# A context tile loaded by one transfer instead of two, with a new instruction order, in an attention and feed-forward kernel

## The chip, the cores and the metric

The kernel runs on one core of a Trainium2 chip. The metric is the device time of one execution in microseconds (us). Its engines are named as in the profile: PE (matrix multiplication; PEld is its weight load), DVE (vector), ACT (activation), POOL (general purpose), SP (here it only issues transfers). Each engine works through its own list of instructions in order and waits on semaphores for the others.

## What is computed

The reference, cut to what matters: x has 8 batches of 512 rows of 512; the context has 64 rows of 512 for each batch.

```python
xn = layernorm(x)
scores = einsum('bsd,bmd->bsm', xn, ctx) / sqrt(512)
attn = softmax(where(mask, scores, -1e30))
x = x + einsum('bsm,bmd->bsd', attn, ctx)          # 0 where a batch has no valid row
z = layernorm(x)
linear_bit(z, w, g) = act_quant(rmsnorm(z, g)) @ ternary_quant(w).T
h = silu(linear_bit(z, w1, g1)) * linear_bit(z, w2, g2)      # 2048 wide
x = x + linear_bit(h, w3, g3)
```

act_quant scales a row by its largest absolute value and rounds to 8 bits; ternary_quant needs the mean of |w| over the whole matrix (1 M values each) before a single weight can be rounded.

## The kernel before, in words

The head of the program brings the weights into shape. Each weight comes as four pieces of 1 MB (load_w, L315; tiles raw). measure_w (L339) sums |w| of each piece (L353), PE adds the partial sums over the partitions (pm, L363), DVE turns the mean into a scale (ws, L366 to L371). quantise_w (L379) scales and rounds a piece (tq, L386 on POOL or L387 on ACT), PE turns it (pw, L396), DVE clips it into w1T, w2T or w3T (L390). arctanh (L423) computes a factor from the mean in many instructions on one column (L434).

Per batch there are three stages. pre (L543) normalises x (statistics L560, t L582/L586), splits it into two float16 halves (xh: cast L590/L591, rest L592), transposes them (xT; on PE for batch 0, by a DMA transpose, L298, for the others), and multiplies by the context (psc, L602). expo and post (L631, L651) do the softmax and add the readout (po, L683; L691). quantise_x (L701) normalises again (xm, L721/L725), multiplies by g1 and g2 (z, L736), finds the largest values (zf, L741), rounds (L799/L800) and transposes (zT). Then, for each of four row blocks, gate and up (L891, L903) multiply by w1 and w2 (L883), apply Silu (L899), multiply both (L927), square (L932) and multiply by g3 (L940); the result is reduced (L964), rounded (L997/L999), transposed (hT) and multiplied by w3 (pd, L825) some blocks later. The last block ends in L854 to L866.

The context of a batch is wanted twice, on partitions 0 to 63 and again on 64 to 127, since the second half serves the low float16 part of the readout. load_x (L469) issues it: `both` (L473) holds the contexts of two batches and serves measure_mem (L489), which finds their scale; `mem` (L475 to L479) holds the one context in both halves; split_mem (L528) turns mem into `ms` (L533 on ACT, L536 on DVE) and its transpose mT. mem has two buffers, x and raw and h share nine large ones (BIG), matmul results share three buffers of two PSUM banks (mm).

The order of the work is written out. The Python code records operations (op, L108), many with several engines to choose from, each with cost estimates in ns; a string (ORDER, L151) holds a compressed list of numbers, each an operation and the engine it goes to, and Plan.order (L128) reads it. The numbers of the cost estimates are not used when the kernel is built: order and engines come from the string alone. All plain loads and stores and all DMA transposes are issued by SP, one after the other.

Of the kernel before, what the change touches and what calls it, by code (L numbers as in the profile page):

```python
# [87 lines left out]
class Plan:  # L88
# [19 lines left out]
    def op(self, engine, cost, run, writes, reads, table=None, other=()):  # L108

        me = len(self.ops)
        deps = set()
# [6 lines left out]
        for b, part in map(pair, writes):  # L120
# [28 lines left out]


ORDER = """  # L151
c-jTQedKy+q5$yo@|^eQob#M>o^#G~UY3@Y?~m_~mM$$_y0o;kv@~?-($LV*(9*qHS{k~vG&D4{S3{SEhW==1XlUqOEnONKS{fQ!8d_R
f`lF@cem)c>QkVi1q!1OQa#WtmQU!`oMe2nrQ4#8uDpMg<p<+~=s!|CmNu{VXm7(g?h3-;Ux=r<{4%MJ;G^9VFn$&>8^oJCphZLbl)KB
QIs2bI$BlOqQXH=A4QFnSkPpCEZhMrOz>R;$BHKS(ikp3k-r{2;TdPnW47@egL)RZ03-%}GdPUq+oHKxy0p8h*^p%V0+dQewtLMQ1TsV
V)Wzo3^a#XxpWQ*?p;mIh3b7MT(a8N>j3L1RXw-=p{Roc*3AOvpr-1O0nuNmu9$^C!AWpXey_!mMb-PPqkprr%*Ubed_<Ev7~{=~pJkZ
0Ri1qA~lR+jN|%(;Yg&beSYW*c4M>a!i{E*)DzLip+}b(F-QR9=Ir51R3xy^M>s(HRc0m!@S4TnI7}X_L&$vWJ};b**!O4TA;z?K^#n&
&zKqaCG$R00DopWU?}$3-?42lWV&F)WWk#4vtKhgFl7ep$Kb$p_&!)MBQ^ozY>OX&HS-12VaM#JV8b@qEz@PMpv||~5m<vUn1LO$Wko^
aCZG(COj`I0GY1J42|qA@W0LF!U?Ihh#2x#0Ce3DqP|vVX$g(t>74FQF*@7IK6CTW-&9i_lu<r;vP-HL6ci_NEY>7RxW%k5Y*n%(xXZF
HY*(10}PjF=mTv0fI8(U-VY@L0uG4Nz7;2rJ^y22a&p8@13um?9#1!e9eA+E>)`2z0Xw*Ye~PzM99!oB4l0Dv?&aaB$PPbtPNK%A>_ge
wV45OPB<#X%6^5QuVft}HY_f;)3>xSmiEk{kv^Xo6pHRiVUPI09CH;#yo^7zrWBa#yL!i*f`2uFV~U92W%(?#k7<SN<rxfF<_|R$PbsB  # L160
}egRsliclL|=0UzQzxPE%$p)<N^O8oP-#^6}#LUdBeTRJ09{+zR!&XN<jQXXbL?J2zx#zr}-Oa^E>X&J(N(0^J_6KKe&z9<wHKhzo=^=
%lG&sAK~Xhf`4*Rekj)ksOI<-KjQLyLn!haf$&42z>m3=^eRq;_xKWj;?v?n_#I#8D`JK3^Plofe!_LcwKU>q!XNpiu#sv)34P8d<drb
yqvH2`SBwZV{wy@a8$ac5%8Qtk@5)p7nxFGnEs1~Q-wG*t!T(HH^G$T;FG5@dVp-hqq7s$P{FZ<4P#MVyk&-AeE{S4HxbR8wA&zAzUIi
jH#gsUa3sPK&sX3`7hT=_#t9RiS!c%-zcOp^$A^Z;?5!+}iHlz=Qw(ufVq;G_s&=J~VUTR86-3v)!DZNTn=_noLln|2+;#`V}C;292#J
!jok78Dwi0`N;aVi$XAH<nxh#gcxTdANH#f4;xWz<4dloQYLT`H<j-bqNgihmW~RjVSBKS%$k?xlxx7i;1ag>p@*i#HKSJuxEN(nr!vh
SCg0Wl`#jL>h=UIU)7rP(l)x=VDD>iVJZi-sOy(lp<0~p2~HpE;r=0e34U9T1v}TIG0y)QNqfvq>}WI`_hL}TPjPhN>(CrSzX9ixg&*2
Oxdaf={t!iznAAqMCnOcxuWLesM1ina#dX@Z8-{uQd7yxDWxFil(aID{#(i@9i=aK<gz@Kwn|r7$}?#o$F(M`$O&zyY~+?wmACR(+AD9
AfzpCE*oOt>Tlo%qN?tiAOXVqNbV^C<M`ZwCAW(Afr0mqVvX>J|Q7$U4@Tu%oQ7b8Z<y|=st4awbmG_i{`o8jO1;CnekSTbANv*E56{v
l#i116)hC>Cykz&B9V#6`?;7mEg2b{pH{+SZO3q;xzifRP@#Guqr<<ylDQKRZcIjC#ptfaK08iz4BR8ug8x>gz{;8jVf8TF!+VMZINSv
3QbFsDw{u^KUE))3aziB*B2mW5bLs|DD%(pnWpv<0leqgq$z*3|k4)?o)`wGo`c9=xhE*i@rhPMgDmwm?O=REc&{=h|0lRXeLoxPoJ?0  # L170
axnhYC|t-6Rn}H;Z5DZnYz&S@T9fWwR(UL?V_HwwmMgP>Jiqoi~iK^YF?{reU;M3`a^AMPnFVMwSoE#>{;K!7j0nuL7i&9)7n~7k7+<(
YfCMvU$lw7(^pzYn`wKitmX8LCh9NxN9tC4)puGJMGdI$^@85gUW~og(%;oO#zBjtiZ<1OwnSI`sLl1fo<LpgW38yCQ4OuoK>If%hYnT
-mGp!DiT0iz(`Wk8s-uTK)ZW*t`c-@CBdv=*GHzPWC>eGAu61;zxAh(x=rz5suTc`+^sY|yzJc`{%A<u2QNyg8OTDM}Q4!V5ve7_yv_Y
ThuLd%PsAAl8${6W2V}w?E+8CpOvC-?spY)-D(EuIwlO8hwI_o2YLIotEszFfPc%YOqb+&rK*rFY37zn9G(wG`!BWs4}N3=&X<AC0vjd
MnEb7kzDxr2>Y^f1;&!rU1f<ELor#L&;s-pQGw`80rWMa0OPWAlQbd9pG_28+hTpiE>goTr&JW=_tSm`(G0ls7&!n#RE(=2r$~wT*9#q
&YYC#?CC5cV}rFjlZCi@q_VK1DHkgYV6H|fh}y7%!3)4cOzmpEMmQwM>C6W#@ULRB`dVr=Bqh1TV~8mSUKD=KQ`lf*F2e@m<c_pr}VNF
v4Ax&o7T{}SShP&rOc5zvcAM2zFH5bgVScxD&mZp#}S;h($@c)bF*d*&4u-axiL$4ZPu-f)x~GCY%Z<5wJ@XB*4*HgRj^*H9$uOYe6xy
H%PQcDSv4zG*ID8|zM4;`V<qv;Y+Ds`Y^^Y~?xtvMth@Ca>lGtwh__b7{kipO?W_;no>RtA9JgxtVXmzz9^t+-z`wv-JjRs!u%h<U+Tj
WYZrpycpP0fDe!&2%7~vEy*$ErthF!K}IE@KD;HG`EYwi)Z>^QFD(3!Y<+`vh@iCcJWPw~*6;I<9yh%>{l_Qp=zqI<%3dyUUH?xbw!?%
gXE?Hj)1ihaQer(^#E*WIz*#!H8?M>eu!Hnyj3%X!D{+65ch8GGgy?TMYWR}ONg_80b-_Q3hhox8uW+m2^1?5#a?4$jdH?U56)tM<|9*  # L180
-N`_FWiAmIcNK1pWMEEv6t@2so5+0TN}GccW)o;tG#lg4safJ+DW;hbF>@o*-1KQH{)Df=s<#;g7fNp=5(B#({!)y8z<|eoR|~3H+SOX
owZYRpLWZ=IKOi9<m$9tL~`!U!Op+BEmCr_ZplrPo||{mE+)h&J7u@%v`N>!yK6T?D$c--xF0wnIg`3mAjIvvQTL5IAaC6w>9|9;;f&m
koAjE_kZj!xp~=pT5|8A)lvg4n@^A|t^2X%p=E#y1y$Z>a7lJ)NN?w`7T#>BF$Q!%Fi@Ph*AyxA4WJ79BjWo#AOSoIo@V+IX_h&Npnq=
i2$jpn7rZ*uiZ|!ZpDd~C@zvsP@wzu<sK{{TS{G3$%e<GiFSCS-s67hNjcqx+fY41kvMDmVg?xnq`_aG+%y|TCW1|IS&-i!AnLvP_tJn
Ub*S1;zxNZiYKDSzozy<dA9@8Hcz&O3Sw67gGp+CO=}^={tTi}?w!?p;0NXZ*MR!EgI_Z|mp$xZm*~-j5#b1Apvi{m@VNHNWfce9^!9M
<4n<KkDE7sh<c=e&5ggg&-Nc_!Ix^&-`*w@aKLpDEeRdU;7RJKm5JF@+-l+e$#*WpZfphm;Gum^3%c7uLWzL3NC&o*!Z&m1li#3Hv=)q
1tb^;Fff93&<Z9&JHSCScnNU03Fbj0Bw;5AgKiKBJ`VmEd=e~zT@VdlgJm!bQo%kL1?lh*<b&^nQt-Fn9^8UNI0%#BBcQ`)z=cv+4>I8
}Yy_h)8^UlJyo9+h7L3DkxC&4>3Ae%9Fdm$Od{_x*;WRu4^Dq`(f-qc!)vy*e!g|;YTVXuxhN-X}_QF4eg|Htk!(zAzOW`WqhU@SU?!t
X|3{T-X{D0au@s|
"""  # L190
# [953 lines left out]
```

## Time and profile before

| | |
|---|---|
| runs | 428.87 us median of 3 (427.7 to 428.94) |
| profiled execution | 427.9 us, of which the profile's span is 425.8 us |
| PE busy | 388.8 us (91%), 2174 matmuls |
| DVE, ACT, POOL busy | 369.0 us (87%), 341.3 us (80%), 368.7 us (87%) |
| granted TensorE clock, mean | 0.987 |
| read from memory, written | 25.76 MB, 8.39 MB |
| the chain that ended last | 78% PE, 6% DVE, 6% POOL, 3% DMA |

The profile is of one execution. Its page gives the busy time of each engine, the span in 40 slices (tenths of a slice, clock, transfer rate), and groups of instructions by line of the kernel with their mean duration and what they waited for; the trace behind it gives the same for any stretch, and instructions in order of time. Idle time on an engine that doesn't set the end costs nothing.

### The profile page before, as it was taken

The numbers are of one execution on the slowest core, as the hardware profiler recorded it, in microseconds if no ns is written. First come the engines' busy times: TensorE is split into PE (matmuls) and PEld (weight loads), VectorE is DVE, ScalarE is ACT, GpSimd is POOL, SyncE is SP. The second block draws the span as 40 slices with busy tenths as digits, with TensorE's granted clock in tenths as the row PEclk, the third lists the DMA queues.
The fourth block names the chain that finished last, engine by engine and source line by source line (L and its number), as shares of the span: only waits on it lengthen the run. The fifth ranks groups of instructions, "written<-read, shape, count | busy, mean of one in ns | idle before, by whom it ended". The sixth has DMA issues, their size and how long they took to land.

```text
span 425.8 us, 6677 instructions
## 1 busy us (share of the span) xinstructions
PE 388.8 (91%) x2174; PEld 192.8 (45%) x2174; DVE 369.0 (87%) x832; ACT 341.3 (80%) x464; POOL 368.7 (87%) x330
## 2 busy tenths in 40 slices
PE   0563878999999999999999999999999999999996
PEld 0341534544444544454445444544454444444444
DVE  4689999999998998799989998999789888897772
ACT  1799999979899799598996898988686986774531
POOL 1789998998999999699999999999699979988650
PEclk9996899999999999999999999999999999999999
DMA  7999994497555578863589635864644546533272
GB/s 217 408 406 376 380 208 52 103 255 147 126 112 150 99 131 157 183 174 68 104 158 276 136 76 82 171 174 83 134 76 148 75 87 146 152 77 73 49 207 90
DMA packets 142514, 67.35 MB, mean 158 GB/s; under 512 B 133136, under 2 KB 133520, under 8 KB 140048
## 3 DMA queue, kind: packets, MB, share of 16 engines
q1 hardware_dynamic: 142480, 66.93, 63.4%
q8 instruction: 17, 0.28, 0.3%
q14 instruction: 17, 0.14, 0.1%
HBM read 25.76 MB, written 8.39 MB: 80 GB/s over the span
## 4 chain that ended last, share of the span: by engine, by line
PE 78%; DVE 6%; POOL 6%; DMA 3%; issue 3%; ACT 2%; SPq 0%; DVEq 0%; POOLq 0%; ACTq 0%
PE p L883 48%; PE pd L825 24%; PE po L683 3%; DMA zT<-xm 2%; PE psc L602 2%; POOL tq L386 2%; DVE st L560 1%; DMA both<-in_ctx_dram 1%; PE pd L854 1%; POOL t L586 1%; POOL xh L592 1%; POOL mv L291 1%; DVE zf L741 1%; DVE h L927 1%; ACT h L899 1%
## 5 line engine op out<-in xcount | busy, mean ns | idle before, releaser
L883 PEld LDWEIGHTS <-zT 128*128 128x128 f16 x1024 | 99.5, 98 | 122.0 <-issue 3.0
L940 POOL TENSOR_TENSOR h<-h,g_bc 128x1024 f32<-128x1024 f32 x55 | 130.4, 2377 | 2.7 <-ACT sq L932 2.1
L883 PE MATMUL p<-w1T,zT 128*128 128x512 f16 x512 | 120.4, 383 | 2.4 <-DVE zT L309 1.5
L883 PE MATMUL p<-w2T,zT 128*128 128x512 f16 x512 | 119.2, 379 | 1.1 <-DVE h L927 0.9
L825 PE MATMUL pd<-w3T,hT 128*128 128x512 f16 x496 | 117.8, 379 | 0.0
L927 DVE SCALAR_TENSOR_TENSOR h<-p,zf,h 128x1024 f32<-128x1024 f32 x64 | 81.9, 1280 | 14.9 <-PE p L883 8.4
L899 ACT ACTIVATE h<-p,zf 128x1024 f32<-128x1024 f32 x64 | 70.1, 1105 | 24.8 <-PE p L883 17.0
L932 ACT ACTIVATE sq<-h 128x1024 f16<-128x1024 f32 x64 | 67.2, 1050 | 17.0 <-DVE h L927 14.8
L825 PEld LDWEIGHTS <-hT 128*128 128x128 f16 x496 | 47.9, 98 | 55.6 <-DMA hT<-h 0.2
L964 DVE TENSOR_REDUCE hf<-h 128x1 f32<-128x2048 f32 x31 | 70.6, 2278 | 1.8 <-POOL h L940 1.7
L736 POOL TENSOR_TENSOR z<-xm,g_bc 128x1024 f32<-128x1024 f32 x29 | 69.8, 2423 | 1.4 <-ACT xm L725 0.6
L997 ACT ACTIVATE h<-h,hf 128x2048 f16<-128x2048 f32 x23 | 45.8, 1994 | 0.2 <-DVE hf L968 0.2
L741 DVE TENSOR_REDUCE zf<-z 128x2 f32<-128x1024 f32 x32 | 38.8, 1211 | 5.8 <-POOL z L736 5.7
L592 POOL TENSOR_TENSOR xh<-t,xh 128x512 f16<-128x512 f32 x32 | 37.3, 1168 | 2.0 <-DVE xh L591 1.2
L799 ACT ACTIVATE xm<-z,zf 128x512 f16<-128x512 f32 x42 | 28.1, 709 | 0.7 <-DVE zf L760 0.7
L731 ACT ACTIVATE xsq<-x,xf 128x512 f32<-128x512 f32 x32 | 22.9, 715 | 6.5 <-DVE x L691 6.0
L835 DVE SCALAR_TENSOR_TENSOR x<-pd,hf,x 128x512 f32<-128x512 f32 x31 | 23.1, 744 | 3.0 <-PE pd L825 2.6
L691 DVE SCALAR_TENSOR_TENSOR x<-po,mx,x 128x512 f32<-128x512 f32 x32 | 22.9, 745 | 1.3 <-PE po L683 1.2
L602 PE MATMUL psc<-mT,xT 128*128 128x128 f16 x256 | 19.7, 224 | 1.9 <-DMA xT<-xh 1.9
L560 DVE BATCH_NORM_STATS2 st<-x 128x6 f32<-128x512 f32 x32 | 21.3, 679 | 0.0
L602 PEld LDWEIGHTS <-xT 128*128 128x128 f16 x256 | 16.9, 101 | 8.5 <-DMA xT<-xh 3.5
L291 POOL TENSOR_TENSOR hf<-hf,neg_half 128x1 f32<-128x1 f32 x32 | 20.1, 634 | 0.2
(134 smaller groups left out, 483.4 us busy)
## 6 DMA issues: line engine op xcount, KB each, us to landing
raw<-in_L_ffn_w_dram SPq DMA_DIRECT2D x10, 1024.0 KB, 13.8
x<-in_x_dram SPq DMA_DIRECT2D x7, 1024.0 KB, 6.9
out_dram<-x SPq DMA_DIRECT2D x7, 1024.0 KB, 4.1
mem<-in_ctx_dram SPq DMA_DIRECT2D x16, 128.0 KB, 6.5
w3T<-in_L_ffn_w_dram SPq DMA_DIRECT2D x2, 1024.0 KB, 12.6
both<-in_ctx_dram SPq DMA_DIRECT2D x4, 256.0 KB, 8.2
x<-in_x_dram SPq DMA_DIRECT2D x2, 512.0 KB, 6.1
g_bc<-in_L_ffn_g_dram SPq DMA_DIRECT2D x1, 1024.0 KB, 14.9
```

The costliest lines, as they stand in the source:

```text
L592: rest = lambda e, t=t, xh=xh: e.tensor_tensor(xh()[:, 1, :], t(), xh()[:, 0, :], ALU.subtract)
L602: T.matmul(psc()[:, c, :, :].rearrange("p s m -> p (s m)"), xT()[:, k, :], mT().rearrange("p (s d) m -> p d s m", s=2)[:, k % ND, :, :], s ...
L736: gain = lambda e, xm=xm, z=z: e.tensor_tensor(z(), xm().broadcast_to([P, 2, D]), g_bc(), ALU.mult)
L741: lambda i=i, z=z, am=am: V.tensor_reduce(am()[:, i, :], z(), AX.X, ALU.max, apply_absolute_value=True),
L825: T.matmul(po(), hT()[:, n * P : (n + 1) * P], w3T()[:, n, :], start=(n == 0), stop=(n == NH - 1),)
L883: T.matmul(ps()[:, k * HC : (k + 1) * HC], zT()[:, g * ND + d, :], weight(d, j * HW // HC + k), start=(d == 0), stop=(d == ND - 1),)
L899: lambda: A.activation(h()[:, j * HW : (j + 1) * HW], ps(), AF.Silu, scale=fac()[:, 0:1]),
L927: lambda: V.scalar_tensor_tensor(cols(), ps(), fac()[:, 1:2], cols(), ALU.mult, ALU.mult),
L932: lambda: A.activation(sq(), cols(), AF.Square, scale=(RMS / H) ** 0.5, accum_out=col(j)),
L940: run = lambda e: e.tensor_tensor(cols(), cols(), g3_bc()[:, j * HW : (j + 1) * HW], ALU.mult)
L964: lambda: V.tensor_reduce(col(2), h(), AX.X, ALU.max, apply_absolute_value=True),
L997: op(ACT, 1995, lambda: A.activation(hq(), h(), AF.Copy, scale=col(5)), [h], [(f, 5)], other=[(POOL, 1970, lambda: G.tensor_scalar(hq(), h ...
```

## The change

There are three parts. First, the two transfers of 64 partitions each become one, whose source names the same 64 rows twice. Second, the order string is another one; its text is left out here. Third, some cost estimates change, which has no effect on the program by itself.

```diff
@@ load_x
         mt = plan.buffer(att, "mem", [P, D], F32, 2, f"mem_{b}")
-        for half in range(2):
-            op(DMA, (475, 650, 364, 500),
-               lambda half=half: Q.dma_start(mt()[half * M : (half + 1) * M, :], mem[b]),
-               [(mt, half)], [])
+        op(DMA, (475, 650, 700, 500),
+           lambda: Q.dma_start(mt(), mem[b : b + 1].broadcast_to([2, M, D])),
+           [(mt, 0), (mt, 1)], [])
@@ load_w, constants, quantise_w: estimates
-            op(DMA, (475, 650, 2750, 1400), lambda k=k: load(k), [raw[i, k]], [])
+            op(DMA, (475, 650, 2620, 1400), lambda k=k: load(k), [raw[i, k]], [])
...
-               other=[(POOL, 1970, lambda by=by: by(G)), (DVE2, 1700, lambda by=by: by(V))])
+               other=[(POOL, 1970, lambda by=by: by(G)), (DVE2, 1275, lambda by=by: by(V))])
...
-        op(DMA, (475, 650, 730, 800), lambda g=g, src=src: Q.dma_start(g_bc()[:, g, :], ...
+        op(DMA, (475, 650, 1160, 800), lambda g=g, src=src: Q.dma_start(g_bc()[:, g, :], ...
```

In the built program the source of a mem transfer, before, is 64 rows of 512 values, twice; afterwards it is 2 copies (step 0) of 64 rows (step 512) of 512 values, and its destination 128 partitions of 512 values.

What the new order does, told from the lists of instructions of each engine:

- SP: both, half of x, mask, half of x, mem, then w1's pieces (second, third, first, fourth), w2's four pieces with the two g_bc transfers among them, the next batch's mem, x and both, three pieces of w3, mem and x of batch 2, the last piece of w3, x of batch 3, both, mem of batch 3, the transposes mT and xT of batch 1, then g3. Before: mask, both, the two halves of mem and x in turn, w1, g_bc, w2 and g_bc, x and mem of batch 1, two pieces of w3, both, a piece of w3, g3, x of batch 2, the last piece of w3, mem.
- ACT: ms of batch 1 (L533) stands ahead of the last half piece of w2's measure; xm of row block 0 (L725) is made here and no more on POOL.
- DVE: one piece of w1's measure (L357), 11 more products h by g3 (L940, 20 for 9), 6 more products z (L736, 9 for 3), 4 rests xh (L592, none before); fewer small columns.
- POOL: 44 for 55 products L940, 23 for 29 products L736, 28 for 32 rests L592; more small columns.
- PE: the same instructions in a slightly other order; the first scores of batch 1 (L602) stand ahead of the fourth turned z of batch 0 and of the sum pm of w3.

More of the change, by code (lines that the diff above doesn't have):

```diff
@@ L151 @@
 ORDER = """
[L152 to L186, printed above, removed]
@@ L187 @@
-1tb^;Fff93&<Z9&JHSCScnNU03Fbj0Bw;5AgKiKBJ`VmEd=e~zT@VdlgJm!bQo%kL1?lh*<b&^nQt-Fn9^8UNI0%#BBcQ`)z=cv+4>I8
-}Yy_h)8^UlJyo9+h7L3DkxC&4>3Ae%9Fdm$Od{_x*;WRu4^Dq`(f-qc!)vy*e!g|;YTVXuxhN-X}_QF4eg|Htk!(zAzOW`WqhU@SU?!t
-X|3{T-X{D0au@s|
+c-jrp{pYf2q5$ygzVGXPf4lDY>wXy;S{nMHhn9wh9$H#jS~@gzXlQAUmWCdh)f^2C4GlfCe4nGCb2RirLqkJDOG8UTOG`sTOG6J04GsO
+!(qZ@WH+%qqAPhK=1189WEGU8qD1j&_fHJ^90s%M?EpQ=XpaUwP4Z0u%UV<~h5q<Ck;$Q&21_^+OB=`oTfJyuXR6z|OAQ3~b1a;6Sz5o
+rd0xmHI0g(n*B1B9;n0SY1f(&?0M2IzbMWl%l)gz`LN@R!)h!I<`16g8B4Tv8=oX8OeFeH8kN01<{;0E%<h&X`}%~50GPJBrehzD^8Md
@@ new lines @@
+AUb#NUV+F`-JtmY7n2{DFYv8I%b?%n6Q!#B)+2>%@UTWSXoH4Z<X=1SY>FYQ&8CklYa)8c{hiAe+R3$dD4%B38ta*wT4&PBqCk(IVG`N
+oC0t#8imv5CyVJ1k`_$pORHFOukRH$r<?`StGk-h>DP5DoRDDC>f)&@QHds#mG9@BO5RZzaryg4mOw;{FqvieKHTb)R<0?|4SBNmrIgu
+*o0+rK&9b=`i87C8Q7+V)Ti(ZvJ2zXf*g}E_;>OZ*@H`RN%g1>^=G&y`&5H^f-7o3HmNZjz&o>m3F-tl<c=J|FG+$<QV(WNCfOyt5&s~
+Ia80GC9``eurcx|aGZbKdA}26QtzewJlUFiFCD=SQf*b1p$u+!@KavFsvVba5Te#zY!)~bzOH(CkN0q4~RiXA&l{!!xeg{ufj=sSfwTE
+Xa0xwhv{u*xJ0iI!zhIAQbS&qK)d3r}@>Gz>TUtj{3=qkLzqj-c@DhYdZj-7KKu~9nDBKlW!ndaC6+ovORku~WG9iwmj6k>W$Pv{y9=o
@@ new lines @@
+TBNXRr?6q!09SdJgY!&rj(R(`Ii}nts3n-JsWOlRoo3HpILpXLO6cQ%9OpxBP>u(ic8M16ZTi41{yK%y95VOK?HI!C>}5cUVgZGgxTT8
+}<dgWbX8m?$TTK!gT1jm@2zsVoZX0O-Gp~bEdD%O}fy1_Qn7PLCDNl69xieW}L((=-)CJCYdt(#F|V1vrLOgF_?LxD{Kg+nH4=^<IIE)
+!z&#U5c>|DW7hPXEwTT>bXg=<m;w7oCg8?wn|YUsb2X+T4Cz-)ft&IZcE>ijBGYB2?2w)DJ;vn1LZ3M@118KxgoB8=e=wgiIj$=_q@UR
+<JD^Vt&kUIg*ArxB#5B1vW3e+P!u^ezGdC9Td2Yunm@RW=qTHU13U9DC;m)2oQ;u<I^kAzT$L*O57h=zx#2wfWA7)GFEp{y=d6Vx8AFw
+rU!hFjf**Y6#(|n3Qu?-f;W&SJXC-yF3zRvZzJdd~vpFvqP=0jY8kFjZP%`eytmqS?I2tz*Lv)mJR7gpSgJ@5-|zy<P>tDq4-=O03XTX
@@ new lines @@
+RYI$ZxnRO37uE<WBsaTku=q&ZoG~5W#J^BA=EITo2J)k$dn<{<rdxYjGux6Uy9;yK)C%$TfI^?{Iex@@;M^kGMV>2$BE<j(>1SC<;~Kd
+v454xT7%Te#J|CS!fCoz9f|RCn3tm_?Q61i7*v1d|Vg`S^gyany>OXzQtn^3Y?ggcS4O1#F0?v6Fd}~yd)0AoczAf=8@RpYeHTwiz9I_
+%!G<q7ZbvV!cJ-lbFt5trLi!RpZEd)SN;tpDa_?x<j?q*d`id&bs;IHg@%|D7NR8Og|@I1=fXmWiWi|N#l*7^7cCJ<SD_;9rGk(aS7KA
+FiU+AJhQzQq7T*>_N<>_XDKRG|q`bHhqiRiD$Sui~mO@6%NLle?u^?8Zq_h&k%3A7+Me!m6tt*wpqx4GLNLMi{oWz0H5zk^*yvb0$iFf
+fNy%gILA;r|5be2N$UH*3zc_LmUC~c*wSdeF8AYG-09F`xVD@pQO(wkC5UdmfBqQs=I^n_w^O4^A~sTxr!D#zuR5|=n7Aw#Vw=cT>)JE
@@ new lines @@
+<?X<(xE>;>rNME7hc)0hAX~SMJC~DJ?amvK&?V(oTMoR&qiaNF%9ZbR<bx%PFO94CRg7RmM_D8p|)`fzng@#zdM*B{{7uq$l~P<dvZ^l
+9$p%UMpcVL|;oQ=>vHn{~#CDjdGB?#t2p9qg<6=%MJOYY~{XkmOE-eF_orVRFLwHGEvS7R^C%KYE>zz7o{bSl&w<LYD!$~s#j$$jg^^N
+R&L6Z(lD~hRFTw~vQWxuQq3q!1*3|xQZ6#5%~ho4lqa=j)RmdhPy+Nqj-Z7qX<Kz}w3LJTT#KQj`hnI{+e$*+DH%16zEL_#U(KVGx-b$
+bucy_$5=AwXQx8gA`!6+w{-mb0f?7a#C8OolrkX-Eb*C257**94YG@y;J5<nt`nft(P4%H5ZLii*UOS<zhSj#(KrJna_NcC!+DN^sWA&
+zfq%74oYNC~TR}ZM5t<|u0Qk&XYZEHpChAwJOd#G5$dItg2wF6B?5v`~7?WHkMWBM;>f<_ubQ`FJM_8rYoTmKQ6C}K|4s5Z3&{deja%~
@@ new lines @@
+4-FXk%@GCfXXs^{#e77wxER&;xb!ueFo5MIkMwUA3rr&=Y#kj%yS9ra`pOrutXfAGD*M)E`<&o9Q9FqRs4tmeS|iSzBr=?WPy?e`;Ip$
+>vZ=PwNFEsY&|(Xant;IoF5UT}OJ#Sm-;gtUvUoVd}v67FBehclERpH>)}}puW^sM$y=7EhDV2jgav$8hT*x`uFzUKIs+nJFThz6-D(x
+g+|y2sSzV<MD&f3G=celder!{+0y&^laVu?OwJhVFZI0f%oyn@Go#0ij4?2t^op_4tM)`s7-O?)mW;JN&}(|z*l0B~tZwwJJ~ndtMK2p
+o^I)I#i7_;;dPLnCk^#-{bz}_8gxNApBWr$Pq|LTjH?w+OhgQbi8In0PGmdEmX42rynmsip=3cMcd*fiFtf|Ran(3MaE9+n@ZRMP!F*8
+Tj$;g>kV{X1_-i(piFpE~+d{}wMG)vaq*jiyTu*%lL99sobvWn)>KAE4IVQc1mW}5cW?3pX`wGHfzc{a}W+RRv6^JimcR;-;BvO3PiF4
@@ new lines @@
+<k@Y-0Nd^I#6_wskb$Gt1`HMpnaq>BOywbu~Y-qE^c)+dZpqy=@Kcs+F`l*2L;s7qe-<vhHTzncL5-mJO_LoPx8k7f#j+?17WFZsyWi+
+Bs`!J<OW*o%NNqvX0i!s#|kwW(7{e8ae}OV<nv@=VU>9VTGKtwX#>v-U{0n=VD#0wG*)=`xBe9D|XaD_RV_RK3Gw^=xm&r9k(C$*6G+G
+dt|Ten_Y6kIO1&VvU9iY_SQ}~CH%~}I!QZ@%Q)_&oCv--VW;M#>;~RBRVQs{?6i}&>(0nY;EEHtMH@K0({P&3-f7~o^QDu-EBsGq>OkD
+W1^bHE_&E-_ard=zbUw$Q;Iq?mZ#Zkma30G}0du(PLMMZfb8tR(viRX7T!5o^i0{~Revd~ujoVJrec%c%;)yHaF~-ijZrh#W4tDX-&Dl
+lwxjVr<caBSL#v8dy+{GbW#aS=F8(hZ=e06L1gpYWKf%|t%yFcN+8+P~jf_pgamfeawb?YwYX57F#;F;TSJFev3+&<RarmNw(J8&az$c
@@ L190 @@
+wsT7kE!N<}TcvYvCC#d0}tqzH+nf-9=vBEqmX&5ija(-IZJMa^A#~y{h}n`@}Qdn%nU<9(FD7;bL#@ZM{EwQ?KUj+>M*?_wK>%dT|eWX
++P;Nyw@)FIWObyy`vlWXZMwt@KWA8-qO3cbua9{>*c-w_72|4%lbuc=JmXYfArSg&g*->_lMru8+fn1kstL(-Y?#tyt|k7+WyTOdojP|
+_56<i@Gjoihkns7`<x&0Oa9ca_`v_b@B5N}^Q->M|ImN(L2&m!_nUs)pZhQf2Q7c&|HbD5<l|uL@BEY>1dZTFfA63CgP->!ffStmX7Iu
+<_^lusT>P&8EExJ%za9K0hzFU#^d~+FmVP$q1-YOT^n-k`^1DGPcsF<o)_yUl1`mG_n87e82ce)6)Ph7%59UEKSOlqH6pVvqunH!@G?)
+ed0-6=-7X
 """
@@ L1018 @@
     for g, src in enumerate((g1, g2)):
-        op(DMA, (475, 650, 730, 800), lambda g=g, src=src: Q.dma_start(g_bc()[:, g, :], src.partition_broadcast(P)),
+        op(DMA, (475, 650, 1160, 800), lambda g=g, src=src: Q.dma_start(g_bc()[:, g, :], src.partition_broadcast(P)),
            [(g_bc, g)], [])
```

## Prediction

> **What bounds the kernel now.** I read the 40 slices first, then busy time by stretches, the instructions in order of time, the waits, and the transfers. The slices:
>
> ```profile
> PE   0563878999999999999999999999999999999996
> DVE  4689999999998998799989998999789888897772
> DMA  7999994497555578863589635864644546533272
> GB/s 217 408 406 376 380 208 52 103 255 147 126 112 150 99 131 157 183 174 68 104 158 276 136 76 82 171 174 83 134 76 148 75 87 146 152 77 73 49 207 90
> ```
>
> A slice is 10.6 us. From the eighth on PE is full. It idles in the first 76 us, where the weights are measured, quantised and turned, and in these slices the transfers are full as well. The stretches put numbers to that (us busy of each stretch; clock, DMA share and GB/s last):
>
> ```profile
> 12.00:20.00 8.00, 4.14 (x36) 3.25 (x36) 4.77 (x15) 7.01 (x8) 6.26 (x8) 1.00 1.05 408
> ...
> 40.00:52.00 12.00, 8.85 (x86) 6.02 (x84) 11.48 (x23) 11.10 (x10) 11.56 (x13) 0.74 1.02 404
> 52.00:60.00 8.00, 6.53 (x40) 3.11 (x38) 7.93 (x26) 8.00 (x14) 7.30 (x12) 1.00 1.23 231
> ```
>
> Columns after the length are PE, PEld, DVE, ACT, POOL. Two things are to be seen: the 16 DMA engines move 404 to 408 GB/s at a share of 1, that is 25.4 GB/s each; and DVE, ACT and POOL are over 90% busy between 30 and 60 us, so the head has two limits, the loads and the vector engines. From 76 us to the last matmul at 422.2 PE has 1.1 us of idle time in all (0.93 of it in 100 to 120), so what follows the head can hardly get faster, and every us by which the head gets longer or shorter ends up in the time.
>
> Where the loads meet the head:
>
> ```profile
> 60.12 0.39 PE L363 MATMUL pm<-part,mean_w 128*128 128x5 f32 x2 [0.24 <-ACT w3T L353]
> 61.59 0.62 PE L602 MATMUL psc<-mT,xT 128*128 128x128 f16 x8 [1.09 <-DMA xT<-xh]
> 62.05 1.89 PE L883 MATMUL p<-w1T,zT 128*128 128x512 f16 x8
> ```
>
> These are instructions in order of time. The first scores of batch 1 (L602) already wait 1.09 us for a DMA transpose (xT), and PE works in order: whatever stands behind that line on PE slips with it.
>
> ```profile
> raw<-in_L_ffn_w_dram SPq DMA_DIRECT2D x10, 1024.0 KB, 13.8
> mem<-in_ctx_dram SPq DMA_DIRECT2D x16, 128.0 KB, 6.5
> both<-in_ctx_dram SPq DMA_DIRECT2D x4, 256.0 KB, 8.2
> g_bc<-in_L_ffn_g_dram SPq DMA_DIRECT2D x2, 256.0 KB, 11.8
> ```
>
> Transfers (count, KB each, us to landing): 1 MB takes 2.6 us at 404 GB/s, yet lands 13.8 us after its issue, so some 11 us of transfers are queued ahead of it. What holds up the queue holds up everything behind it.
>
> **Part 1, the merged transfer.** Sixteen mem transfers of 128 KB become eight of 256 KB. Eight issues go, each 0.47 to 0.57 us on SP where SP doesn't wait (0.5 × 8 = 4 us); SP is not on the path, so I count 0. Without that cover, at most the first issue counts: 0.5 us.
>
> The bytes stay the same; how they are dealt out may not. The new source is written as 2 copies (step 0) of 64 rows of 512, so its outermost count is 2. In every plain transfer of the trace the outermost count is 64 or more (the g_bc rows repeat one row 128 times: outermost count 128), and those keep 16 engines busy. No row has fewer pieces than engines, so I bound it from both sides:
> - lower end, as both: 262,144 B over 16 engines, 16,384 B each / 25.4 GB/s = 0.64 us, as now. Cost 0.
> - upper end, one copy to each of two engines: 131,072 B each / 25.4 = 5.15 us. These two engines fall 5.15 − 0.64 = **4.5 us** behind per transfer, and each later load lands only when its share on them has.
>
> By bytes the nearest row is both, by its outermost count no row is near. I take the upper end, as an estimate: all rows that reach 25.4 GB/s on each engine have enough outer pieces for 16, and this transfer has two to give.
>
> Here a page speaks against the change. The Trainium skill, "DMA: Bandwidth & Descriptors", section "Rules for kernel authors", says that an outermost dim of size c under 16, such as a leading zero-stride broadcast of c copies, confines the whole DMA to at most c engines; by it the price is the upper end, 4.5 us, and without it 0; no run here shows it yet.
>
> What the upper end does. In the new order mem_0 stands before all weight loads, mem_1 behind w2, mem_2 before x_2 and the last quarter of w3, mem_3 before the first transposes of batch 1. Before, the loads through mem_3 are done at about 54 us (rate falls to 231 in 52 to 60). In the new order g3's 1 MB stands behind them instead of among them: −2.6. So 51.4 + 4 × 4.5 = **69.4 us** until the two engines have let all four pass. The transpose xT_0 is queued behind and needs another 1 to 2 us: about 71 against 61.59, so PE's L602 slips by 9.5 us, and with it pm of w3, the w3 turns and all down matmuls.
>
> The way there fits: ACT has ms_1 (L533) ahead of the last half quarter of w2's measure. mem_1 ends 10.8 MB of loads; at 204, 408 and 401 GB/s in the first three stretches of 10 us that is about 32 us, plus 2 × 4.5 = 41. The w2 mean (36.18 before) then comes at about 43, +7, of which 3 us were idle in ws anyway (pm 36.18, reciprocal 39.27).
>
> Given back: PE idles some 3 us between 62 and 78 for DVE and ACT; while PE waits they work ahead: −2. Added: four transfers (batches 4 to 7) later, each up to 4.5 us in front of transposes, which stood on the path at zT (0.93 us of waiting now): 0 to 1.5 each, I take 0.5: +2. Sum: 9.5 − 2 + 2 = **+9.5 us**.
>
> **Part 2, the new order.** Moved from POOL to DVE: 11 products h by g3 (2377 to 1293 ns) and 6 products z (2423 to 1348). Four xh rests (POOL 1168) go to DVE too, a form with no row there: between the cast at 429 and L536 at 1122, I take 750, near L691's 745 with the same 512 elements; both ends differ by under 2 us in sum. One measure of w1 goes from ACT (1897) to DVE, price as L964 (2278). Many columns of 0.2 us go from DVE to POOL. Net: POOL about −38, DVE about +15, ACT about +6. DVE goes from 369 to some 384 of 426 us. PE hides that: from 76 us it sets the pace. If that cover fails, a late L927 keeps one of three PSUM buffers, at 0.4 to 0.5 us a wait.
>
> In the head, xm_0 goes from POOL to ACT, so the first z product starts after the third tq and one ph product (0.43) and not after xm (0.69) as well: about 31.4 against 32.54, 1.1 us. But DVE was busy 17.67 of 18.50 us between 34.94 and 53.44, and gets more work there (w1T done with 4 us more in sum): I count 0, between −1.1 and +1. w1's start: x is issued one place earlier, hidden by w1's last quarter (ACT waits for it at 20.12). g3 moves behind the first transposes: its first reader (DVE, L940) started at 67.17, so it is hidden unless the queue is as late as in part 1, and then by the same slip. The tail has the same last work, 64 down matmuls (13.8 us) ahead of the last turn instead of 60: 0.
>
> **The sum** goes against the profiled execution, 427.9 us (span 425.8 and 2.1 around it): 427.9 + 9.5 = 437.4. The median of the runs is 428.87, 1.0 above that execution, so the time is **438.4**.
>
> **Rivals.**
> - A, forecast, 438.4. Its own range: only the first transfer's 4.5 us reach the end minus 1 (432), to all 18 of four transfers reach it (446). Chance 0.74.
> - B, the copies spread over 16 engines and the order does nothing: 428.9. For it: both, with the same bytes. Chance 0.09.
> - C, not slower: they spread, and the head gains 1.1 at z_0 and the 0.9 wait at zT: 427.9 − 1.5 + 1.0 = 427.4. It decides if the engine count is 8 or more: then a transfer takes at most 262,144 / 8 / 25.4 = 1.3 us, three times 0.65 late, which the new order's spare covers. Against it: DVE is full there. Chance 0.11.
> - D, they spread, but DVE, at 90%, frees PSUM late at some batch borders: 4 × 0.5 = 2 us, 431. Against it: POOL is relieved by twice as much. Chance 0.06.
>
> About 0.3% (1.3 us) is what can be told from no change. Faster is C, 0.11; same is B, 0.09; slower A and D, 0.80. The range of 8 in 10 takes A (nine tenths of it), D and most of B: 428 to 446.
>
> **What would show it.** A: the GB/s row has slices far under 376 in the first 60 us (two engines move 51) and loads reach past 60 us; ACT waits for mem at L533; mem lands later than 6.5 us; L602 of batch 1 waits for xT, near 71 us; PE is full some 10 us later. B and C: GB/s stays near 400 until 50 us. The step most likely to be wrong is the count of engines; next, how much of 18 us reaches L602.

## The result, and the profile after

The changed kernel takes 457.78 us (median; 456.84 to 459.81) where the kernel before, on the same chip, takes 428.88 (427.7 to 428.94). The ratio is 1.0687, with a 95% interval of 1.0645 to 1.0729: 28.9 us slower, where 9.5 had been forecast. The direction and the mechanism were right, the size was off by a factor of three. The span of the profiled execution is 455.1 us.

The slices of the kernel after (one is 11.4 us; PE, DVE, DMA busy in tenths, then the rate):

```profile
PE   0563662999989999889998899999999999999996
DVE  4767853799998999979999799999979999999973
DMA  7999649673975373989349963747764345726443
GB/s 233 373 345 332 228 153 145 166 172 76 158 99 116 92 178 69 108 182 221 69 94 111 220 155 69 150 85 198 137 95 103 116 93 127 106 83 118 90 145 109
```

Before, four slices moved 376 to 408 GB/s and PE was full from the eighth. Now no slice reaches 376, PE falls to 0.2 in the seventh (68 to 80 us), and DVE has a hole at the same place. There is a second kind of loss: eights on PE in the middle of the run, where before there were only nines. The same three stretches as before (us busy of PE, PEld, DVE, ACT, POOL; clock, DMA share, GB/s):

```profile
12.00:20.00 8.00, 3.12 (x28) 2.55 (x29) 4.88 (x16) 3.49 (x5) 1.65 (x3) 1.00 1.05 365
40.00:52.00 12.00, 4.77 (x18) 2.39 (x19) 8.34 (x33) 7.71 (x11) 7.82 (x10) 0.61 0.71 235
52.00:60.00 8.00, 5.84 (x77) 4.92 (x76) 8.00 (x16) 7.97 (x9) 7.66 (x9) 0.94 1.03 331
```

Between 40 and 52 us DVE, ACT and POOL were 92 to 96% busy before and are 64 to 70% busy now: they have become waiters. Where the transfers went is seen in slices of 0.5 us between 60 and 80 us:

```profile
DMA  8984111111111111499119911111122099996996
GB/s 234 283 213 152 70 41 45 57 66 49 49 49 66 49 49 49 138 185 81 45 45 49 58 49 49 49 49 53 49 41 25 18 228 38 237 543 262 524 524 262
```

For two long stretches the 16 engines are one tenth busy and move 49 GB/s. Two engines at 25.4 GB/s move 51. This is two engines working off their queue while fourteen have nothing to do. PE, in order of time (start, us, work, idle time before it and what ended that):

```profile
46.09 0.59 PE L363 MATMUL pm<-part,mean_w 128*128 128x5 f32 x2 [7.59 <-ACT w2T L353]
...
78.24 1.04 PE L602 MATMUL psc<-mT,xT 128*128 128x128 f16 x8 [7.42 <-DMA xT<-xh]
79.07 1.06 PE L304 MATMUL pt_z<-ident_h,xm 128*128 128x128 f16 x8
79.92 0.54 PE L363 MATMUL pm<-part,mean_w 128*128 128x5 f32 x2
```

The mean of w2 comes at 46.09 for 36.18, the first scores of batch 1 at 78.24 for 61.59, the mean of w3 at 79.92 for 60.12. ACT's waits say why the first is late (total, times, longest):

```profile
ACT ms L533 <- DMA mem<-in_ctx_dram: 8.4, 2, 4.4
```

The wait of 4.4 us is for the mem of batch 1 and ends at 44.28; the last half piece of w2's measure stands behind it on ACT. And the transfers as the page has them (count, KB, us to landing, where one was recorded):

```profile
raw<-in_L_ffn_w_dram SPq DMA_DIRECT2D x10, 1024.0 KB, 15.5
x<-in_x_dram SPq DMA_DIRECT2D x7, 1024.0 KB, 18.1
...
mem<-in_ctx_dram SPq DMA_DIRECT2D x8, 256.0 KB
...
both<-in_ctx_dram SPq DMA_DIRECT2D x4, 256.0 KB, 10.8
```

Everything that shares the queue lands later (both 10.8 for 8.2, raw 15.5 for 13.8).

### The profile page after: what moved, and what is told of

It is laid out like the page before. It is cut to its first block, busy times and chain, and to the rows that moved or that the text cites. A ratio compares the mean times of both kernels' runs of the same rounds, so it can differ in the third digit from the quotient of the medians.

```text
span 455.1 us, 6652 instructions
## 1 busy us (share of the span) xinstructions
PE 396.7 (87%) x2174; PEld 199.3 (44%) x2174; DVE 386.5 (85%) x782; ACT 347.7 (76%) x473; POOL 342.5 (75%) x342
## 4 chain that ended last, share of the span: by engine, by line
PE 62%; DMA 14%; DVE 11%; SPq 6%; POOL 3%; issue 2%; ACT 1%; DVEq 0%; POOLq 0%
PE p L883 37%; PE pd L825 20%; DMA x<-in_x_dram 6%; SPq L322 4%; DVE h L927 3%; DMA mem<-in_ctx_dram 3%; DVE hf L964 2%; PE psc L602 2%; PE po L683 2%; DMA mT<-ms 2%; DMA xT<-xh 2%; DVE h L940 2%; DMA hT<-h 1%; SPq L1019 1%; POOL h L940 1%
## 5 line engine op out<-in xcount | busy, mean ns | idle before, releaser
L883 PE MATMUL p<-w1T,zT 128*128 128x512 f16 x512 | 122.5, 387 | 2.9 <-DVE zT L309 1.1
L940 POOL TENSOR_TENSOR h<-h,g_bc 128x1024 f32<-128x1024 f32 x44 | 105.3, 2396 | 4.9 <-ACT sq L932 3.3
L736 POOL TENSOR_TENSOR z<-xm,g_bc 128x1024 f32<-128x1024 f32 x23 | 56.1, 2445 | 3.1 <-ACT xm L725 2.1
L997 ACT ACTIVATE h<-h,hf 128x2048 f16<-128x2048 f32 x24 | 48.0, 1999 | 6.6 <-DVE hf L968 6.5
L592 POOL TENSOR_TENSOR xh<-t,xh 128x512 f16<-128x512 f32 x28 | 34.0, 1217 | 5.6 <-ACT xh L590 3.2
L799 ACT ACTIVATE xm<-z,zf 128x512 f16<-128x512 f32 x45 | 30.6, 712 | 2.5 <-DVE zf L760 2.2
L602 PE MATMUL psc<-mT,xT 128*128 128x128 f16 x256 | 21.2, 236 | 12.7 <-DMA xT<-xh 7.4
L940 DVE TENSOR_TENSOR h<-h,g_bc 128x1024 f32<-128x1024 f32 x20 | 28.9, 1451 | 1.3 <-ACT sq L932 1.3
L602 PEld LDWEIGHTS <-xT 128*128 128x128 f16 x256 | 18.5, 107 | 19.3 <-DMA xT<-xh 7.7
L291 POOL TENSOR_TENSOR hf<-hf,neg_half 128x1 f32<-128x1 f32 x32 | 21.6, 677 | 6.5 <-DVE hf L955 6.3
## 6 DMA issues: line engine op xcount, KB each, us to landing
raw<-in_L_ffn_w_dram SPq DMA_DIRECT2D x10, 1024.0 KB, 15.5
both<-in_ctx_dram SPq DMA_DIRECT2D x4, 256.0 KB, 10.8
```

The lines of the kernel that those rows point to most:

```text
L592: rest = lambda e, t=t, xh=xh: e.tensor_tensor(xh()[:, 1, :], t(), xh()[:, 0, :], ALU.subtract)
L602: T.matmul(psc()[:, c, :, :].rearrange("p s m -> p (s m)"), xT()[:, k, :], mT().rearrange("p (s d) m -> p d s m", s=2)[:, k % ND, :, :], s ...
L736: gain = lambda e, xm=xm, z=z: e.tensor_tensor(z(), xm().broadcast_to([P, 2, D]), g_bc(), ALU.mult)
L883: T.matmul(ps()[:, k * HC : (k + 1) * HC], zT()[:, g * ND + d, :], weight(d, j * HW // HC + k), start=(d == 0), stop=(d == ND - 1),)
L940: run = lambda e: e.tensor_tensor(cols(), cols(), g3_bc()[:, j * HW : (j + 1) * HW], ALU.mult)
L997: op(ACT, 1995, lambda: A.activation(hq(), h(), AF.Copy, scale=col(5)), [h], [(f, 5)], other=[(POOL, 1970, lambda: G.tensor_scalar(hq(), h ...
```

## The experiments

All compare with runs of the kernel before on the same chip (its median lies between 428.7 and 428.9 us on every chip, so the runs can be compared with each other too). "New order" is the order string of the changed kernel. L533 and L602 stand a few lines lower in some of them.

### Is it the transfer or the order? (e1, e4)

e1 keeps the new order and gives it the old transfers:

```diff
-        op(DMA, ..., lambda: Q.dma_start(mt(), mem[b : b + 1].broadcast_to([2, M, D])), ...)
+        def bring():
+            for half in range(2):
+                Q.dma_start(mt()[half * M : (half + 1) * M, :], mem[b])
+
+        op(DMA, ..., bring, [(mt, 0), (mt, 1)], [])
```

> The new order, with each context again in two transfers of 64 rows (issued one after the other where the merged one stood). Theory T (the merged transfer goes over two engines and is the whole loss): the time falls from 457.8 back to 427 to 431, no ACT wait for mem at L533, L602 of batch 1 near 62 us. Theory O (the new order has a share of its own: ms ahead of the last half measure of w2, g3 behind the transposes, DVE with 15 us more): it stays above 433; if the order were all of it, near 457.

Measured: 429.01 us, ratio 1.0009 (0.9982 to 1.0036). The order alone does nothing that can be measured, and the whole loss goes with the merged transfer. PE in e1:

```profile
36.74 0.39 PE L363 MATMUL pm<-part,mean_w 128*128 128x5 f32 x2 [4.26 <-ACT w2T L353]
58.77 1.03 PE L604 MATMUL psc<-mT,xT 128*128 128x128 f16 x8 [2.21 <-DMA xT<-xh]
```

These two starts, 36.74 and 58.77, are what the other runs of the new order are measured against below. e4 is the fourth corner, the merged transfer in the old order:

```diff
+        brought = []
+        def bring():
+            if not brought:
+                Q.dma_start(mt(), mem[b : b + 1].broadcast_to([2, M, D]))
+            brought.append(b)
         for half in range(2):
-            op(DMA, ..., lambda half=half: Q.dma_start(mt()[half * M : (half + 1) * M, :], mem[b]), [(mt, half)], [])
+            op(DMA, ..., bring, [(mt, half)], [])
```

> The old order, with the merged transfer issued where the first of the two halves stood. Theory T with two engines and nothing else: loss as in the new order, near 457. Theory P (the new order makes the delay dearer, since ms of batch 1 stands ahead of the last half measure of w2 on ACT, so the mean of w2 and all that follows wait for mem): the loss here is clearly smaller, 435 to 447, and the mean of w2 (L363) is at its old place near 36 us.

Measured: 464.04 us, ratio 1.0845 (1.0801 to 1.089). For the time as a whole theory P falls: the loss is some 35 us in the old order and 28.8 in the new one, so the new order makes it cheaper and not dearer. In the head P holds: the w2 mean comes at 40.50 here (4.3 us late, for 9.4 in the new order) and L602 at 77.55 (16.0 late, for 19.5). So more than half of the old order's loss comes after the head; after 80 us PE's longest waits are 5.2 us for zT, 4.4 for xT and 2.7 for hT. Why the later transfers cost more there was not tried.

### Is it the number of engines? (e2, e9, e10, e11)

e2 exchanges the two source dimensions, so that row m lands on partitions 2m and 2m+1. e9 to e11 keep the copies outside and raise their number (k = 4, 8, 16), each of the first 32, 16 or 8 rows alone. The four don't compute what the kernel should; they are there for their time:

```diff
-           lambda: Q.dma_start(mt(), mem[b : b + 1].broadcast_to([2, M, D])),
+           lambda: Q.dma_start(mt(), mem[b].rearrange("m (o d) -> m o d", o=1).broadcast_to([M, 2, D])),   # e2
+           lambda: Q.dma_start(mt(), mem[b : b + 1, 0 : P // k, :].broadcast_to([k, P // k, D])),          # e9, e10, e11
```

> One merged transfer of the same 256 KB with the same step of 0, only the two source dimensions exchanged: 64 rows outside, 2 copies inside. Row m then lands on partitions 2m and 2m+1 instead of m and m+64, so the contexts stand on the wrong partitions; the work is the same. Theory T (the outermost count of 2 decides): 427 to 431, as with two transfers, and GB/s near 400 in the first 40 us. Theory Z (reading each row twice with step 0 is itself slow, or a 256 KB transfer is): it stays near 457.

> One merged transfer of 256 KB whose source is 4 copies (step 0) of the first 32 rows, in place of 2 copies of 64: outermost count 4. Rows 32 to 63 of each context are thus replaced by rows 0 to 31. Theory E (as many engines as the outermost count; each falls behind by its share): 262,144 / 4 / 25.4 = 2.58 us, 1.94 behind a spread one, against 4.52 with two; loss in proportion, 28.8 x 1.94 / 4.52 = 12.4 on top of 427 to 429: 439 to 442. Theory N (anything with a step of 0 outside goes over two engines, or over one): 457 or more.

> As before with 8 copies of the first 16 rows: outermost count 8. Theory E: 1.29 us on each of 8 engines, 0.65 behind, loss 28.8 x 0.65 / 4.52 = 4.1: 430 to 433; below that where a delay of 0.65 is hidden. Theory N: 457 or more.

> As before with 16 copies of the first 8 rows: outermost count 16, all engines. Theory E: no loss, 426 to 429 as with 64 rows outside (426.4). Theory N: 457 or more; a part of it if a step of 0 outside has a price of its own.

| source, outermost first | us | ratio (95%) | w2 mean, us | L602, us |
|---|---|---|---|---|
| 2 copies, 64 rows (changed kernel) | 457.78 | 1.0687 (1.0645 to 1.0729) | 46.09 | 78.24 |
| 4 copies, 32 rows (e9) | 439.14 | 1.0264 (1.0234 to 1.0295) | 41.74 | 68.28 |
| 8 copies, 16 rows (e10) | 434.14 | 1.0119 (1.0084 to 1.0155) | 38.18 | 62.30 |
| 16 copies, 8 rows (e11) | 427.44 | 0.9978 (0.9961 to 0.9994) | 36.12 | 57.85 |
| 64 rows, 2 copies (e2) | 426.36 | 0.995 (0.9933 to 0.9968) | 35.84 | 56.46 |

The bytes moved, the number of transfers and the step of 0 are the same in all five. The outermost count differs, and the time falls with it. (How many different rows are read differs too, but e2 reads all 64 and e11 only 8, and both are fast.) Theories Z and N fall: a step of 0 outside costs nothing at a count of 16. e10 lies a little above the 430 to 433 expected of it.

The engines can be counted in the traces, which record when each engine has done its share of a transfer. Each of the eight mem transfers has 16 such marks in e11 and e2, but one early mark and then 2 in the changed kernel, 4 in e9 and 8 in e10. The piece of w1 that the changed kernel issues right behind mem of batch 0 is done on fourteen engines by 11.69 us and on the last two at 17.54 and 17.72. The rate says the same (e9, slices of 2 us, 0 to 80):

```profile
DMA  0939999999999999999999999992299396990639
GB/s 32 293 108 337 300 266 388 409 410 409 410 410 402 408 408 434 399 285 291 343 433 421 446 408 335 244 173 102 107 98 102 73 79 197 393 262 0 131 75 224
```

From 54 to 62 us the rate is 98 to 107 GB/s: four times 25.4 is 102. With two copies it was 49. The Trainium skill, "DMA: Bandwidth & Descriptors", section "Rules for kernel authors", has this as a rule (an outermost size c under 16 confines a transfer to at most c engines; a multiple of 16 put outermost is the cure); the runs with 2, 4, 8, 16 and 64 agree with it. The same table advises one transfer of 128 partitions in place of two to disjoint halves. Here that depends on how the one is written: 426.4 with the rows outside against 429.0 for two, but 457.8 with the copies outside.

### Which transfers cost it? (e3, e5, e6, e7, e8)

The new order, with the merged transfer for some batches only and two halves for the rest:

```diff
+        def bring():
+            if b < 4:      # e3; e5: b >= 4; e6: b == 0; e7: b == 1; e8: b in (2, 3)
+                Q.dma_start(mt(), mem[b : b + 1].broadcast_to([2, M, D]))
+            else:
+                for half in range(2):
+                    Q.dma_start(mt()[half * M : (half + 1) * M, :], mem[b])
```

> The new order, merged transfers for batches 0 to 3 only, two transfers of 64 rows for batches 4 to 7. Theory T by its trace: full PE began about 20 us later in the head and some 9 us of new stalls came after 100 us. If these stalls belong to the later transfers, this run is near 448; if they are a consequence of the late head, it stays near 457. By the forecast's sizes (head 7.5, later 2) it would be 436 to 437 on top of the new order.

> The new order, merged transfers for batches 4 to 7 only. If head and later batches add up (19.9 us for 0 to 3, measured as 448.9 against 429.0, and the rest of 28.8 here): 438 (436 to 440). If the later loss exists only because the head is late (the later work is then closer to its transfers): 430 to 432. The forecast had 0.5 for each of the four: 431.

> The new order, merged transfer for batch 0 only, the first in the queue. Theory of equal shares (each of the four in the head puts 4.5 us on the end, as the forecast took it): 433.5. Theory S (what costs is a mem transfer behind which something on the path waits; batch 0 has slack until the weights are there): 429 to 431.

> The new order, merged transfer for batch 1 only. ACT makes ms of batch 1 (L533) ahead of the last half measure of w2, so the mean of w2 and the factor of all w2 pieces wait for this transfer. Equal shares: 433.5. Theory S: one delay of 4 to 5 us at the w2 mean, L363 near 41 instead of 36.7, and most of it at the end: 432 to 435. If the later issue of x of batch 2 (SP waits there for a buffer of a raw piece that tq frees) adds to it: above 436.

> The new order, merged transfers for batches 2 and 3, which stand ahead of x of batch 2, the last piece of w3 and the first transposes. Equal shares: 438. Theory S: mem_2 is issued some 12 us ahead of the next load and hidden, mem_3 delays the transposes by 4.5 us: 433 to 435. If SP, which issues in order, is held up by the two full queues: 437 to 441.

| merged for batches | us | ratio (95%) | above e1 | w2 mean | L602 | between them |
|---|---|---|---|---|---|---|
| none (e1) | 429.01 | 1.0009 (0.9982 to 1.0036) | | 36.74 | 58.77 | 22.0 |
| 0 (e6) | 435.99 | 1.0177 (1.0133 to 1.0222) | 7.0 | 43.12 | 67.05 | 23.9 |
| 1 (e7) | 435.09 | 1.0148 (1.0126 to 1.0171) | 6.1 | 40.98 | 64.28 | 23.3 |
| 2, 3 (e8) | 437.74 | 1.0204 (1.0175 to 1.0233) | 8.7 | 36.19 | 67.32 | 31.1 |
| 0 to 3 (e3) | 448.93 | 1.0479 (1.0457 to 1.0501) | 19.9 | 46.49 | 78.4 | 31.9 |
| 4 to 7 (e5) | 437.05 | 1.019 (1.0144 to 1.0236) | 8.0 | 37.16 | 59.10 | 21.9 |
| all (changed kernel) | 457.78 | 1.0687 (1.0645 to 1.0729) | 28.8 | 46.09 | 78.24 | 32.2 |

The parts nearly add: 7.0 + 6.1 + 8.7 = 21.8 against 19.9 for the head at once, and 19.9 + 8.0 = 27.9 against 28.8 for all. So the later stalls are not a consequence of the late head; they have their own price, 2.0 us a transfer. In the head nothing is hidden: even a single transfer costs 6 to 7 us. e6 lies above both times expected of it (433.5, and 429 to 431). The starts on PE, e6 first, then e8:

```profile
43.12 0.39 PE L363 MATMUL pm<-part,mean_w 128*128 128x5 f32 x2 [3.92 <-ACT w2T L353]
67.05 1.03 PE L607 MATMUL psc<-mT,xT 128*128 128x128 f16 x8 [3.53 <-DMA xT<-xh]
```

```profile
36.19 0.59 PE L363 MATMUL pm<-part,mean_w 128*128 128x5 f32 x2 [3.70 <-ACT w2T L353]
67.32 1.03 PE L607 MATMUL psc<-mT,xT 128*128 128x128 f16 x8 [7.70 <-DMA xT<-xh]
```

Batches 0 and 1 delay the mean of w2 (by 6.4 and 4.2 us, by 9.4 together), and the stretch after it grows by only 1 to 2. Batches 2 and 3 leave the mean alone and lengthen the stretch after it by 9.1. The two legs are run one after the other. What ties the second to the first is SP, which issues in order. In e1 (start, us of the issue: x of batch 2, the last piece of w3, x of batch 3; then SP's wait at the last of them):

```profile
35.09 0.53 SPq L487 DMA_DIRECT2D x<-in_x_dram  x1
37.11 0.33 SPq L326 DMA_DIRECT2D raw<-in_L_ffn_w_dram  x1
39.92 0.33 SPq L487 DMA_DIRECT2D x<-in_x_dram  x1
```

```profile
SPq L487 <- ACT tq L387: 2.2, 1, 2.2
```

x of batch 3 takes one of the nine large buffers, and SP waits until ACT's tq of w2 has read a piece and freed it; this tq needs the mean of w2. So x of batch 3 is issued 3.2 us after the mean in e1, 3.4 after it in e6 (46.47) and 3.3 in e7 (44.28). Behind it in SP's list stand both, mem of batch 3 and the transposes of batch 1: a late mean makes all of them late.

In the changed kernel SP stands longer, and elsewhere:

```profile
36.94 0.53 SPq L478 DMA_DIRECT2D mem<-in_ctx_dram  x1
37.57 12.31 SPq L485 DMA_DIRECT2D x<-in_x_dram  x1
49.98 1.59 SPq L326 DMA_DIRECT2D raw<-in_L_ffn_w_dram  x1
51.66 0.38 SPq L485 DMA_DIRECT2D x<-in_x_dram  x1
...
53.49 0.73 SPq L478 DMA_DIRECT2D mem<-in_ctx_dram  x1
54.28 15.66 SPq L298 DMA_TRANSPOSE mT<-ms  x1
70.05 3.92 SPq L298 DMA_TRANSPOSE xT<-xh  x1
```

```profile
SPq L485 <- POOL tq L386: 12.3, 1, 12.3
```

The profile puts the 12.31 us at x of batch 2 down to a tq of w2 on POOL. It can't be that: e1 has the same order and issues this x at 35.09, before the same tq begins there at 38.61. What the long issues have in common is a merged transfer close ahead of them. In e7, with mem of batch 1 merged, the issue right behind it takes 6.67 us (0.58 in e1). In e8, with batches 2 and 3 merged and the mean in its place, these two do:

```profile
34.40 6.70 SPq L326 DMA_DIRECT2D raw<-in_L_ffn_w_dram  x1
...
43.83 15.08 SPq L298 DMA_TRANSPOSE mT<-ms  x1
```

In e1 they take 0.33 and 1.30. So a merged transfer holds up not only the two engines but also SP, as the last of the three expectations for e8 has it, and while SP stands the other fourteen get nothing new: from 47 to 50.5 us the changed kernel moves 49 to 66 GB/s. That SP waits for room in the queues of the two engines is likely; no run tests it.

Both delays end in mem of batch 3. Its last share is done at 56.75 us in e1 and at 76.21 in the changed kernel, 19.5 us later, and the first scores start 2.0 us after it in both (58.77, 78.24).

The later price is seen in e5 between 220 and 232 us (slices of 0.3 us), with SP's issues there and what PE then waits for:

```profile
DMA  0099999289950237990199111111111111199999
GB/s 9 10 218 251 235 274 277 47 194 290 289 101 0 48 49 160 172 61 20 55 55 55 55 48 48 55 55 48 48 55 55 48 48 46 33 239 242 289 277 289
```

```profile
222.56 0.56 SPq L479 DMA_DIRECT2D mem<-in_ctx_dram  x1
223.18 1.22 SPq L298 DMA_TRANSPOSE mT<-ms  x1
225.05 5.93 SPq L1007 DMA_TRANSPOSE hT<-h  x2
```

```profile
231.25 1.01 PE L607 MATMUL psc<-mT,xT 128*128 128x128 f16 x8 [2.98 <-DMA mT<-ms]
```

The mem transfer of the last batch keeps two engines busy alone: in 17 slices behind its issue the rate is 46 to 55 GB/s, 5.1 us in all, and 5.15 had been worked out for it. The transposes mT and hT issued right behind it move next to nothing until it is through, and PE loses 2.98 us at the scores that need mT.

### A version that keeps the good part (e12)

e2 leaves the rows on the wrong partitions. e12 makes it whole: from batch 1 on the rows stand interleaved, and the consumers are told so.

```diff
+                Q.dma_start(mt(), mem[b].rearrange("m (o d) -> m o d", o=1).broadcast_to([M, 2, D]))   # b > 0
-    mT = plan.buffer(att, "mT", [P, 2 * ND, M], F16, 2, ...)
+    mT = plan.buffer(att, "mT", [P, 2 * ND, P], F16, 2, ...)
-    flip(mT, ms, mT, lambda: ms()[0:M, :, :]...
+    flip(mT, ms, mT if b else (lambda: mT()[:, :, 0:M]), lambda: (ms() if b else ms()[0:M, :, :])...
-                        mT()...[:, k % ND, :, :],
+                        mT()...[:, k % ND, :, 0 : (P if b else M) : (2 if b else 1)],
-                    plan.buffer(att, "ph", [P, NC, 2, M], F16, 1, ...),
+                    plan.buffer(att, "ph", [P, NC, M, 2] if b else [P, NC, 2, M], F16, 1, ...),
```

> A complete version of the merged transfer with the 64 rows outside, from batch 1 on: row m goes to partitions 2m and 2m+1, ph is written with its two halves interleaved, the whole of ms is transposed (256 KB for 128 KB) and the scores read every second column of mT; batch 0 is loaded by two transfers. The mask bias is kept in bfloat16 and some small tiles have fewer buffers, for room. If only the transfer matters: 426 to 427.5, 0.3 to 0.6% under the kernel before. If the doubled transpose (about 1 us more for each of 7 batches, in the queue ahead of xT) or the strided operands cost: 428 to 434.

Measured: 424.81 us (422.83 to 426.4), ratio 0.9907 (0.9877 to 0.9936): 0.9% under the kernel before, and less than the 426 to 427.5 expected. Its six runs fall into two groups (422.8 to 423.5 and 426.1 to 426.4), and its interval overlaps that of e2 (426.36), so that it beats e2 is not shown. The doubled transposes and strided operands cost nothing that shows. Its slices:

```profile
PE   0665779999999998999999999999999999999996
GB/s 226 409 406 426 361 205 238 101 118 132 136 83 162 106 124 151 211 150 94 94 173 269 108 55 153 99 225 150 69 107 134 76 86 123 176 50 100 74 183 90
```

PE reaches 9 in the seventh slice (before: in the eighth), and the loads run at 406 to 426 GB/s in the second to fourth (before 408, 406, 376). That this is due to fewer issues and earlier loads is read from the trace (w2 mean at 35.79, L602 at 56.35) and was not tried by itself; the mask bias in bfloat16 and the smaller pools were not separated either.

## Why the prediction was right in kind and wrong in size

- **The count of engines** (the step it named as most likely wrong): right. Two engines, 49 GB/s, about 5 us a transfer; the row of both, the rival reading, was not comparable, since its outermost count is 128.
- **The new order counts 0**: right, 0.9982 to 1.0036 for e1. Of the shifts between engines, two were sized well and one not: in e1 DVE has 19 us more than before, ACT 6 more, POOL 25 less, where +15, +6 and −38 had been summed up. The rivals B, C and D fall with the spread they assume. With the transfer spread the new order gives 427.4 (e11) and 426.4 (e2), near C's 427.4; whether by the two gains that C names was not looked at.
- **The w2 mean at about 43, +7**: 46.09, +9.9. The term for mem_0 was mis-sized, 6.4 for 4.5; that for mem_1 was not, 4.2. That ms of batch 1 stands ahead of the measure was read rightly from the order.
- **"Before, the loads through mem_3 are done at about 54 us"**, and with it "51.4 + 4 × 4.5 = 69.4" and "about 71 against 61.59": this step failed. 54 us is where the rate falls, not where mem of batch 3 lands. Its two halves are issued at 48.02 and 49.94 in the kernel before, and the trace has for them (tile mem, 47 to 51 us):

```profile
DMA to landing us min/median/max: 10.7/11.5/12.3
```

They land at 60.28 and 60.65, less than 1 us ahead of L602. The gap into which the first 8.6 us of delay (61.59 − 51.4 − 1.6) were to fall does not exist. By the sum one transfer alone would have cost nothing (51.4 + 4.5 + 1.6 = 57.5, ahead of 61.59) and the two of e8 0.4; one alone costs 7.0 or 6.1 (e6, e7), and those two 8.7. With 60.65 in place of 54 the same sum gives 76.05 until the two engines are through; measured is 76.21, and L602 follows at 78.24, 16.65 late and not 9.5. That it fits so well is in part luck: in e1 mem of batch 3 lands at 56.75, 1.3 earlier than 60.65 − 2.6, and the four transfers cost 19.5 there and not 18. What the sum also leaves out is SP: it takes the loads as a queue that is always filled, while SP's issues wait for buffers that follow the w2 mean and stall behind the merged transfers. So 9.4 us up to the mean and 10.1 behind it add up to the 19.5.
- **"−2.6" for g3**: it did not reach the end. The new order with split transfers has L602 at 58.77, 2.8 ahead of the kernel before, and the same time. So what counts is the delay against e1, 19.5, and not the one against 61.59.
- **"−2 given back"**: no. With the head alone merged (e3) L602 is 19.7 us late against e1, and the end 19.9. DVE, ACT and POOL waited too (64 to 70% busy between 40 and 52 us in the changed kernel) and did not work ahead.
- **"I take 0.5: +2" for the later four**: 8.0 alone, 8.9 on top of the head. The place was right, in front of transposes; the size was taken from a wait of 0.93 us in a trace in which nothing stood in front of them for 5 us.
- The sum: 19.9 + 8.9 = 28.8 us, where 9.5 − 2 + 2 was forecast. Case A's own upper end, all 18 us of the head, left out the later four, and that a transfer can cost more than the 4.5 us by which its engines fall behind.

## What to carry to other kernels

Read the outermost count of both sides of every transfer in the built program, not only its bytes: with 2, 4 and 8 the same 256 KB transfers cost 28.8, 10.1 and 5.1 us against two of half the size, and with 16 nothing. A transfer that holds a few engines delays everything behind it in the queue that needs all engines, small transposes too. Before letting a delay fall into slack, take the landing of the last transfer itself, not the place where the rate falls, and look at what paces the issues in that stretch: if they wait for buffers that the delayed work frees, delays add up. And check what the profile names as the end of a wait against a run in which that work comes later than the issue.

## What the runs showed of the hardware that was not expected

mem_0 alone delays the w2 mean by 6.4 us, more than the 4.5 by which its two engines fall behind. The rates in slices of 1 us from 0 to 40, e6 and then e1:

```profile
DMA  0189549999999999999999999999999999999999
GB/s 0 12 297 330 173 126 311 227 328 332 303 317 285 297 309 342 387 412 403 387 393 412 365 399 416 234 195 342 395 395 404 414 395 248 268 346 397 412 403 397
```

```profile
DMA  0489679899999999999999999999999999999999
GB/s 0 29 289 383 144 118 313 275 209 330 406 412 406 412 408 410 408 406 412 408 412 403 410 410 399 401 410 397 361 410 377 244 266 332 375 436 436 424 401 442
```

From 10 to 16 us all engines are busy in both, but e6 moves about 300 GB/s for 406 to 412. In its records of single packets, those of 2 KB take 100 to 119 ns (medians of each us) in that stretch and 84 ns afterwards, as in e1. So engines that are out of step seem to slow each other: in the six slices from 10 to 15 the shortfall is 601 of 2454, 1.5 us at full rate, most of the 1.9 by which 6.4 exceeds 4.5. The marks of single engines fit this: in e6 fourteen have done their share of the first weight piece issued by 12.22 us, the last two at 17.48 and 18.77, so the slowest is 6.5 us behind. Why the packets are slower was not tried and stays open.
